# A fused vision network on one core: the other image's sums and norms moved from VectorE and GpSimd to TensorE and ScalarE

## The chip, the cores and the metric

The kernel runs on one core of a Trainium2 chip. The time is that of one execution on the device, in microseconds, taken as a median of several runs. A core has TensorE (matmuls into PSUM), VectorE (DVE in the profile), ScalarE (ACT), GpSimd (POOL) and SyncE (SP, which only issues transfers here); each works through its own queue of instructions in order, and semaphores make them wait for each other.

## The reference

Sixteen images of 48x48 tokens with 96 channels go through two layers, each a state-space block and a feed-forward network with a residual:

```python
# layer 0
x = x + ss2d_0(layernorm(x, 1e-6)) # gate, output product, and a branch: expand, 3x3 depthwise conv, reduce, squeeze-excite
x = x + ffn_0(layernorm(x, 1e-5))
# layer 1
x = x + ss2d_1(layernorm(x, 1e-6)) # layernorm of y over 192 channels, gate, output product
x = x + ffn_1(layernorm(x, 1e-5))

def ss2d(x):
    xc, z = split(x @ in_proj_w.T)                 # 2 x 192 channels
    xc = silu(depthwise3x3(xc) + conv_b)
    xs = [rows(xc), columns(xc), rows(xc)[::-1], columns(xc)[::-1]]    # 4 directions
    dt, B, C = split(x_proj_w @ xs);  delta = softplus(dt_proj_w @ dt + dt_proj_b)
    h[t] = exp(delta[t] * A) * h[t-1] + delta[t] * xs[t] * B[t]        # 16 states per channel
    y[t] = sum over states of h[t] * C[t], + Ds * xs[t]
    y = the four directions added, the column ones turned back
    # layer 1: y = (y - mean) / sqrt(var + 1e-5) * g + b
    return (y * silu(z)) @ out_proj_w.T

def ffn(x):   # operands rounded to 8 bits, sums rounded to fp16
    h = relu(q16(q16(q8(x) @ q8(W1).T) + q8(b1)))
    return q16(q16(q8(h) @ q8(W2).T) + q8(b2))
```

## The kernel before

One image's state is kept in DRAM between its three parts, in one of two sets of buffers. Its scan, `scan` (L461), is the bulk of the work: two pairs of directions, three chunks of 768 tokens, three channel groups j, four row groups i, four state groups g, which is 288 steps in each layer and 9216 in all. A step takes a tile of 128 partitions (32 channels x 4 states) by 768 tokens:

- ScalarE makes `a`, the exp of delta times a rate, in PSUM (L497); `a` has two buffers.
- GpSimd makes `b`, delta u times B (L499), four buffers.
- VectorE scans (L532). In three of four steps the result is written over `a`, and VectorE multiplies it by C to `hc` (L534). In the fourth the result `h` goes to SBUF and GpSimd multiplies.
- ScalarE copies the last column to `carry` for the next chunk (L536).
- TensorE adds the states up: two products per step, issued for two steps together, into `py` (L542), which starts from the skip term (L518) and is copied out every 16 steps (L551).

Beside a scan runs the work of another image, written as Python generators. `together` (L799) takes one scan step and then as much of the other work as keeps it in step: every `yield n` of a generator counts n units, `WORK` has the total of each kind, and the other work is to be spent after 0.94 of the 288 steps. A planner then orders each engine's queue by the program's order as priority and by its own estimate of when operands are ready, so that instructions can be placed ahead of where they stand in the program. The stages are, for images in pairs: the scans of layer 0 beside `final(m-1)` and `first(m+1)`, then beside `middle(m)`; the scans of layer 1 beside `middle(m+1)`, then beside `final(m)` and `first(m+2)`.

- `first` (L769): `before` with layer 0: layernorm (`norm`, L277), transposes (`channels_first`, L298), projections, 3x3 convolutions as nine products with diagonal matrices (`conv`, L329), B and C, delta and delta u.
- `middle` (L772): `merge` (L557), `gate` (L575), `branch` (L599), `add_out` (L654), `feed_forward` (L722) with a norm of its own, and `before` for layer 1.
- `final` (L783): `merge`, `centred` (L686), `gate`, two `add_out`, `feed_forward`.

What the change touches computes as follows before it. `merge` adds the four directions of y, three loaded tiles of [128, 2304] with channels in the partitions, by three additions on GpSimd, two of which read a tile turned (rows and columns of the image swapped, L564 and L566), and one after ScalarE has turned a half tile into `low` (L569, L571). `centred` sums y over channels with matrices of ones (L695), VectorE subtracts the mean from PSUM (L700), ScalarE squares (L701), TensorE sums the squares in columns (L706). In `norm`, VectorE reduces (L281, L289), GpSimd subtracts the mean and multiplies by 1/deviation with broadcast operands (L284, L294). `branch` works in three parts of 128 channels; each part's product is evicted by ScalarE with a bias for part 0 (L632) and added to `t2` by VectorE for parts 1 and 2 (L634). `add_out` adds products out of PSUM to x on VectorE: plainly (L672) or scaled by 1/deviation of each token (L676). In `feed_forward` each sixth of the tokens gets: three products and copies to fp16 by ScalarE (L738), bias and relu by VectorE (L740), a cast to 8 bits by VectorE (L742), nine products (L747), a copy to fp16 by ScalarE (L755), and two additions on GpSimd, of b2 and of the residual (L757, L759).

All evictions of the other work go through `pst` (L272), 2 PSUM buffers:

```python
self.big = pool("big", bufs=5)                                  # tiles of 2304 columns
self.work = pool("work", bufs=2)
self.pq = pool("pq", bufs=2, space=bass.MemoryType.PSUM)        # pst
```

## Time and profile before

| | |
|---|---|
| median of 3 runs | 28,072.75 us (28,056.17 to 28,076.98) |
| the profiled execution's own time | 28,053.55 us |
| its span, first to last instruction | 28,051.8 us |
| first scan, last scan | about 199 us after the start, 178 us before the end |
| mean granted TensorE clock | 0.803 |
| VectorE, GpSimd, TensorE, ScalarE busy | 84%, 83%, 76%, 50% |
| DMA engines busy | 44% on average, 157 GB/s |

A line of the groups reads: line of the code, engine, operation, result and operands with shapes, count, then busy microseconds, mean nanoseconds of one, and the engine's idle time just before these instructions with what ended it. A matmul of fp32 operands has two records. TensorE's busy time includes pipelining and a modelled end, and its clock varies with the stretch: 1.00 in the convolutions, about 0.7 where the scan is alone. A line of the waits reads: who, for whom, microseconds in total, how often, the longest. A line of the windows reads: from and to, length, then each engine's busy time in it with the count of instructions, the granted clock and DMA.

Of the 32 stages, those with `middle` take about 861 us, those with `final` and `first` 867 to 881.

### The profile page before, as it was taken

Reading aid. Unit: us, or ns where it says so; the run is one execution under the profiler, and the core shown is the slowest. Engines: PE = TensorE matmul, PEld = TensorE weight load, DVE = VectorE, ACT = ScalarE, POOL = GpSimd, SP = SyncE. Lnnn points to the kernel's source line nnn. Section 1 sums busy time; section 2 is a strip of 40 time slices with the busy share of each in tenths; the row PEclk is TensorE's granted clock in tenths of the full one; section 3 lists DMA queues with packets and bytes.
Section 4 is the critical chain, followed back from the end, with each engine's and each line's share of the span. In section 5 each row is a group of like instructions: output and inputs, shape, how many; then the busy total and the mean of one; then the engine's idle time right before and its main releaser. Section 6 shows DMA issues by size and latency. Waiting matters only on the chain. (4 is left out here: it accounts for less than half of the span.)

```text
span 28051.8 us, 226543 instructions
## 1 busy us (share of the span) xinstructions
PE 21292.3 (76%) x67072; PEld 7663.6 (27%) x67072; DVE 23442.8 (84%) x18375; ACT 14073.2 (50%) x22285; POOL 23212.7 (83%) x13238
## 2 busy tenths in 40 slices
PE   7777777777778777787777877778777787677876
PEld 2222222222222222232222322223222232222322
DVE  5988888888888888888888888888888888888887
ACT  4455544555445554455444554545545455454553
POOL 5888888887888888888888888888888888888887
PEclk7888878887788777787788877788777887778876
DMA  4444444444444444444444444444444444444443
GB/s 165 151 161 168 152 147 161 167 165 154 149 158 164 163 158 146 156 170 159 162 151 152 165 163 161 150 152 165 160 166 147 150 165 163 163 154 150 162 161 110
DMA packets 1062584, 4406.08 MB, mean 157 GB/s; under 512 B 212064, under 2 KB 212064, under 8 KB 1030368
## 3 DMA queue, kind: packets, MB, share of 16 engines
q1 hardware_dynamic: 869792, 3757.78, 38.2%
q10 hardware_dynamic: 191552, 633.81, 5.7%
q8 instruction: 528, 8.65, 0.1%
q14 instruction: 712, 5.83, 0.1%
HBM read 3499.97 MB, written 891.22 MB: 157 GB/s over the span
## 5 line engine op out<-in xcount | busy, mean ns | idle before, releaser
L499 POOL TENSOR_TENSOR b<-d,bc 128x768 f32<-128x768 f32 x9216 | 16563.8, 1816 | 2899.3 <-DVE a L532 2656.7
L542 PE MATMUL py<-hc,fold_sb 128*32 128x384 f32 x36864 | 11193.0, 620 | 5228.8 <-DVE hc L534 4136.5
L497 ACT ACTIVATE a<-d,l_a 128x768 f32<-128x768 f32 x9216 | 8270.9, 904 | 5410.1 <-DVE h L532 2892.7
L532 DVE TENSOR_TENSOR_SCAN a<-a,carry,b 128x768 f32<-128x768 f32 x4608 | 8257.8, 1814 | 1845.1 <-ACT a L497 966.9
L534 DVE TENSOR_TENSOR hc<-a,bc 128x768 f32<-128x768 f32 x6912 | 6408.5, 945 | 269.1 <-PE py L542 61.4
L542 PEld LDWEIGHTS py<-hc,fold_sb 128*32 128x32 f32 x36864 | 2569.4, 124 | 12738.4 <-DVE hc L534 6589.0
L534 POOL TENSOR_TENSOR hc<-h,bc 128x768 f32<-128x768 f32 x2304 | 4191.1, 1819 | 1239.9 <-DVE h L532 1048.5
L532 DVE TENSOR_TENSOR_SCAN a<-a,b 128x768 f32<-128x768 f32 x2304 | 4003.0, 1753 | 1011.6 <-ACT a L497 516.1
L532 DVE TENSOR_TENSOR_SCAN h<-a,carry,b 128x768 f32<-128x768 f32 x1536 | 2761.6, 1798 | 396.0 <-ACT a L497 355.9
L536 ACT COPY carry<-a 128x1 f32<-128x1 f32 x4608 | 714.7, 156 | 3748.9 <-DVE hc L534 3713.2
L342 PE MATMUL pst<-e,dg 128*128 128x384 f32 x5184 | 1777.2, 490 | 0.0
L532 DVE TENSOR_TENSOR_SCAN h<-a,b 128x768 f32<-128x768 f32 x768 | 1337.3, 1741 | 341.3 <-ACT a L497 156.2
L443 PE MATMUL pst<-dts,wpack_sb 24*128 24x384 f32 x2304 | 1378.5, 726 | 147.9 <-ACT dl L444 146.7
L455 POOL TENSOR_TENSOR du<-dl,u 128x768 f32<-128x768 f32 x576 | 1031.6, 1804 | 328.5 <-ACT dl L448 220.9
L342 PE MATMUL pst<-wxa,dg 128*128 128x384 f32 x3456 | 1218.5, 497 | 27.3 <-DMA dg<-taps_l0a 23.1
L342 PEld LDWEIGHTS pst<-e,dg 128*128 128x128 f32 x5184 | 959.0, 189 | 788.3 <-issue 153.7
L444 ACT ACTIVATE dl<-pst,wpack_sb 128x384 f32<-128x384 f32 x1152 | 654.1, 577 | 858.9 <-PE pst L443 685.4
L425 PE MATMUL pst<-u,wpack_sb 128*24 128x384 f32 (+1 forms) x2304 | 890.5, 513 | 37.9 <-ACT row L429 19.3
L342 PE MATMUL pst<-wxb,dg 128*128 128x384 f32 (+1 forms) x2304 | 879.9, 509 | 3.6 <-ACT wxb L374 3.6
L551 ACT COPY yt<-py 128x768 f32<-128x768 f32 x576 | 459.5, 798 | 726.1 <-PE py L542 724.7
L443 PEld LDWEIGHTS pst<-dts,wpack_sb 24*128 24x128 f32 x2304 | 526.4, 260 | 1073.9 <-ACT dl L444 516.0
L342 PEld LDWEIGHTS pst<-wxa,dg 128*128 128x128 f32 x3456 | 623.9, 189 | 622.8 <-issue 226.1
(147 smaller groups left out, 15581.5 us busy)
## 6 DMA issues: line engine op xcount, KB each, us to landing
d<-dd SPq DMA_DIRECT2D x2304, 768.0 KB, 4.6
bc<-bc SPq DMA_DIRECT2D x1536, 768.0 KB, 5.0
dd<-dl ACTq DMA_DIRECT2D x192, 1152.0 KB, 4.7
dd<-du SPq DMA_DIRECT2D x576, 384.0 KB, 2.7
y<-yt ACTq DMA_DIRECT2D x576, 384.0 KB, 2.3
u<-u ACTq DMA_DIRECT2D x96, 1152.0 KB, 4.9
first<-u SPq DMA_DIRECT2D x288, 384.0 KB, 3.1
first<-y SPq DMA_DIRECT2D x288, 384.0 KB, 3.2
```

The lines of the kernel that those rows point to most:

```text
L342: nc.tensor.matmul(img(o[:, :SUB]), lhsT=dg[:n, k, :], rhs=img(p[:n], PW)[:, PQ * q + i : PQ * q + i + PQ, j : j + HW], start=(k == 0), st ...
L425: nc.tensor.matmul(o[:m, :SUB], lhsT=w[:, j, :], rhs=u[j][:, cs], start=(j == 0), stop=(j == 2))
L443: nc.tensor.matmul(o[:, :SUB], lhsT=dtw[:, col, :], rhs=dts[:, cs], start=True, stop=True)
L444: nc.scalar.activation(dl[:, cs], o[:, :SUB], AF.Identity, bias=self.get(t + "dtb")[:, col : col + 1])
L455: nc.gpsimd.tensor_tensor(du, dl[:, cs], u[j][:, cs], ALU.mult)
L497: nc.scalar.activation(a, d[:, 0, :], AF.Exp, scale=rates[:, pair, j, i, g : g + 1])
L499: nc.gpsimd.tensor_tensor(b, d[:, 1, :], bc[:, 0, :], ALU.mult)
L532: nc.vector.tensor_tensor_scan(way(h), way(a), way(b), start, ALU.mult, ALU.add)
L534: (nc.vector if here else nc.gpsimd).tensor_tensor(hc, h, cc, ALU.mult)
L536: nc.scalar.copy(carry[:, at : at + 1], h[:, last : last + 1])
L542: nc.tensor.matmul(py[at : at + 32, q, :SUB], lhsT=self.fold, rhs=hcs[k][:, q * SUB : (q + 1) * SUB], start=False, stop=(g == GROUPS - 1),)
L551: nc.scalar.copy(sub(yt), py[:, :, :SUB])
```

## The change

No part of the scan is changed. Of the other image's work:

- `merge` becomes sums on TensorE, in pieces of 384 tokens: identity times the first tile, plus halves of the identity times turned slices of the others, evicted by ScalarE.
- `centred` no longer calls `merge`: it has a constant `centre` of four 128x192 blocks, identity less 1/192, which merge and centre in one group of four products; ScalarE squares out of PSUM and copies.
- `norm` subtracts and scales by ScalarE, one activation of 96 columns for each of the 18 token groups, with the mean as bias and then 1/deviation as scale.
- `channels_first` casts to 8 bits on ScalarE.
- `branch` adds `t2` by a product with the identity; ScalarE evicts.
- `add_out` adds x by a product with the identity; the scaled products are first scaled by ScalarE into `y2` and added the same way; `final` calls it once instead of twice.
- `feed_forward`: bias and relu on ScalarE; b2 and the residual each by a pair of products and an eviction by ScalarE.
- The units and `WORK` follow: 192, 461, 152 for 201, 464, 151.

```diff
     def norm(self, x, eps):
-        nc.vector.tensor_scalar_mul(m, m, 1.0 / DM)
+        nc.vector.tensor_scalar_mul(m, m, -1.0 / DM)
+        yield 2
         xm = self.bigt([128, NT, DM], "xm")
-        nc.gpsimd.tensor_tensor(xm, x, m.unsqueeze(2).broadcast_to([128, NT, DM]), ALU.subtract)
-        yield 6
+        for i in range(NT):
+            nc.scalar.activation(xm[:, i, :], x[:, i, :], AF.Identity, bias=m[:, i : i + 1])
+            if i % 3 == 2:
+                yield 0.8
...
-        nc.gpsimd.tensor_tensor(xm, xm, r.unsqueeze(2).broadcast_to([128, NT, DM]), ALU.mult)
-        yield 4
+        yield 1
+        for i in range(NT):
+            nc.scalar.activation(xm[:, i, :], xm[:, i, :], AF.Identity, scale=r[:, i : i + 1])
+            if i % 3 == 2:
+                yield 0.8
...
-                nc.vector.tensor_copy(out, p[:DM, :SUB], saturate=False)
+                nc.scalar.activation(out, p[:DM, :SUB], AF.Identity, saturate=False)
...
     def merge(self, s):
-        nc.gpsimd.tensor_tensor(img(y[0][:64]), img(y[0][:64]), swapped(y[2][:64]), ALU.add)
-        yield 5.5
-        nc.gpsimd.tensor_tensor(img(y[0][64:]), img(y[0][64:]), swapped(y[1][64:]), ALU.add)
-        yield 5.5
-        low = self.bigt([64, L], "low")
-        nc.scalar.copy(img(low), swapped(y[2][64:]))
-        yield 1
-        nc.gpsimd.tensor_tensor(y[1][:64], y[1][:64], low, ALU.add)
-        yield 5.5
+        for q in range(NQ):
+            cs, rows = slice(q * SUB, (q + 1) * SUB), slice(q * PQ, (q + 1) * PQ)
+            o = self.pst()
+            nc.tensor.matmul(o[:, :SUB], lhsT=self.ident, rhs=y[0][:, cs], start=True, stop=False)
+            nc.tensor.matmul(img(o[:64, :SUB]), lhsT=low, rhs=turned[2][:, rows], start=False, stop=True)
+            nc.tensor.matmul(img(o[64:, :SUB]), lhsT=high, rhs=turned[1][:, rows], start=False, stop=True)
+            nc.scalar.copy(y[0][:, cs], o[:, :SUB])
+            yield 2
+        for q in range(NQ):
...
+            nc.tensor.matmul(o[:64, :SUB], lhsT=low, rhs=y[1][:, cs], start=True, stop=False)
+            nc.tensor.matmul(img(o[:64, :SUB]), lhsT=high, rhs=turned[2][:, rows], start=False, stop=True)
+            nc.scalar.copy(y[1][:64, cs], o[:64, :SUB])
+            yield 1.4
...
     def branch(self, ya, yb):
+                if m > 0:
+                    nc.tensor.matmul(
+                        o[:DM, :SUB], lhsT=self.ident[:DM, :DM], rhs=t2[:, cs], start=True, stop=False
+                    )
...
-                    nc.vector.tensor_tensor(t2[:, cs], o[:DM, :SUB], t2[:, cs], ALU.add)
+                    nc.scalar.copy(t2[:, cs], o[:DM, :SUB])
...
     def add_out(self, x, terms, scaled=(), scale=None):
+            if scaled:
+                o = self.pst()
+                self.products(o, q, scaled, True)
+                y = self.work.tile([128, TQ * DM], F32, name="y2", tag="w1")
                 for i in range(TQ):
                     at = TQ * q + i
-                    nc.vector.scalar_tensor_tensor(
-                        xq[:, i, :],
+                    nc.scalar.activation(
+                        y[:, i * DM : (i + 1) * DM],
                         o[:, i * DM : (i + 1) * DM],
...
+            o = self.pst()
+            for k, y in enumerate(added):
+                nc.tensor.matmul(o[:, : TQ * DM], lhsT=self.ident, rhs=y, start=k == 0, stop=False)
+            self.products(o, q, terms, False)
+            nc.scalar.copy(xq, o[:, : TQ * DM])
             yield TQ * len(terms) / 2
...
     def centred(self, s):
+            for n, into, sq, at in ((128, y[0], sqa, 0), (64, y[1], sqb, 128)):
+                o = self.pst()
+                for k, rhs in enumerate((img(y[0][:, cs]), img(y[1][:, cs]), turned[1][:, rows], turned[2][:, rows])):
+                    nc.tensor.matmul(
+                        img(o[:n, :SUB]),
+                        lhsT=self.centre[:, k, at : at + n],
+                        rhs=rhs,
+                        start=(k == 0),
+                        stop=(k == 3),
+                    )
+                outs.append((o, n, into, sq))
+            for o, n, into, sq in outs:
+                nc.scalar.activation(sq[:, cs], o[:n, :SUB], AF.Square)
+                nc.scalar.copy(into[:n, cs], o[:n, :SUB])
+            yield 5
...
     def feed_forward(self, t, x):
-                nc.vector.tensor_scalar(h1[:, m, :], h1[:, m, :], b1[:, m : m + 1], 0.0, ALU.add, ALU.max)
+                nc.scalar.activation(h1[:, m, :], h1[:, m, :], AF.Relu, bias=b1[:, m : m + 1])
...
-            nc.gpsimd.tensor_tensor(y1, y1, b2.unsqueeze(1).broadcast_to([128, TQ, DM]), ALU.add)
-            xs = x[:, TQ * q : TQ * (q + 1), :]
-            nc.gpsimd.tensor_tensor(xs, xs, y1, ALU.add)
-            yield 1.5
+            o = self.pst()
+            nc.tensor.matmul(o[:, : TQ * DM], lhsT=self.ident16, rhs=y1, start=True, stop=False)
+            nc.tensor.matmul(o[:, : TQ * DM], lhsT=self.ones16, rhs=b2, start=False, stop=True)
+            y1 = self.work.tile([128, TQ * DM], F16, name="y1")
+            nc.scalar.copy(y1, o[:, : TQ * DM])
+            yield 0.5
+            o = self.pst()
+            xs = x[:, TQ * q : TQ * (q + 1), :].rearrange("p s c -> p (s c)")
+            nc.tensor.matmul(o[:, : TQ * DM], lhsT=self.ident, rhs=xs, start=True, stop=False)
+            nc.tensor.matmul(o[:, : TQ * DM], lhsT=self.ident16, rhs=y1, start=False, stop=True)
+            nc.scalar.copy(xs, o[:, : TQ * DM])
+            yield 1
...
-WORK = {"first": 201, "middle": 464, "final": 151}
+WORK = {"first": 192, "middle": 461, "final": 152}
```

## The prediction

> **What bounds the kernel now.** I read the table of engines first, then the costliest groups, then who waits for whom on VectorE, and last the busy times stage by stage, since the average over the span hides which engine is full where.
>
> ```profile
> PE 21292.3 (76%) x67072; PEld 7663.6 (27%) x67072; DVE 23442.8 (84%) x18375; ACT 14073.2 (50%) x22285; POOL 23212.7 (83%) x13238
> ...
> L499 POOL TENSOR_TENSOR b<-d,bc 128x768 f32<-128x768 f32 x9216 | 16563.8, 1816 | 2899.3 <-DVE a L532 2656.7
> L532 DVE TENSOR_TENSOR_SCAN a<-a,carry,b 128x768 f32<-128x768 f32 x4608 | 8257.8, 1814 | 1845.1 <-ACT a L497 966.9
> L534 DVE TENSOR_TENSOR hc<-a,bc 128x768 f32<-128x768 f32 x6912 | 6408.5, 945 | 269.1 <-PE py L542 61.4
> L534 POOL TENSOR_TENSOR hc<-h,bc 128x768 f32<-128x768 f32 x2304 | 4191.1, 1819 | 1239.9 <-DVE h L532 1048.5
> ```
>
> The kernel is 9216 scan steps. Four steps give VectorE four scans (about 1.78 us) and three products (0.945), 10.0 us, so 2.5 us a step; they give GpSimd five products of 1.82, 2.3 us a step. With nothing else to do a step takes 2.5 us, and VectorE is the bound with GpSimd close behind. 9216 x 2.5 is 23,040 us; the ends without a scan take some 200 us before the first and 178 after the last. The other 4,600 us of the span are what the work of the other image adds, about 145 us in each of the 32 stages.
>
> ```profile
> DVE a L532 <- ACT a L497: 1483.0, 1336, 10.6
> DVE a L532 <- ACT carry L536: 1157.8, 1062, 9.0
> DVE h L532 <- ACT a L497: 512.1, 183, 11.8
> ...
> DVE xs L672 <- PE pst L662: 149.8, 38, 8.3
> DVE y L700 <- PE pst L695: 142.6, 21, 23.6
> ```
>
> VectorE's idle time ends mostly on ScalarE (3.2 ms), seldom on GpSimd. ScalarE is half idle, but its queue is in order: an eviction that waits for TensorE holds back the exp behind it. That is the danger of a change that adds evictions. The stages say where it matters. First a stage with `middle` (columns: TensorE, its weight loads, VectorE, ScalarE, GpSimd busy, then clock and DMA): merge, branch part 0, branch parts 1 and 2, output sum, norm with transposes, feed-forward.
>
> ```profile
> 11462.90:11499.00 36.10, 16.64 (x45) 4.11 (x44) 29.66 (x23) 15.88 (x23) 36.10 (x17) 0.69 0.56 186
> ...
> 11547.40:11608.30 60.90, 57.64 (x196) 23.05 (x196) 56.96 (x43) 30.11 (x58) 53.97 (x34) 1.00 0.40 144
> 11608.30:11753.00 144.70, 142.14 (x511) 64.26 (x512) 137.92 (x108) 73.78 (x134) 124.81 (x73) 1.00 0.45 156
> 11778.40:11820.60 42.20, 38.40 (x161) 22.75 (x160) 31.13 (x30) 14.46 (x17) 26.89 (x16) 0.74 0.37 131
> 11820.60:11853.80 33.20, 21.87 (x71) 7.40 (x72) 32.55 (x30) 15.05 (x17) 30.86 (x17) 0.71 0.34 119
> 11853.80:11921.00 67.20, 42.78 (x156) 11.06 (x155) 63.90 (x59) 29.69 (x56) 55.03 (x37) 0.75 0.30 106
> ```
>
> Then one with `final` and `first`: merge, centring, output sums, norm with transposes, feed-forward.
>
> ```profile
> 13184.00:13210.20 26.20, 12.53 (x39) 3.28 (x36) 23.37 (x18) 14.82 (x21) 26.20 (x14) 0.76 0.62 223
> 13210.20:13263.60 53.40, 45.34 (x152) 21.59 (x152) 40.76 (x39) 20.57 (x41) 43.39 (x23) 0.79 0.43 149
> ...
> 13295.20:13401.30 106.10, 83.02 (x314) 37.53 (x314) 97.54 (x93) 46.20 (x84) 90.73 (x52) 0.84 0.36 126
> 13401.30:13450.90 49.60, 25.96 (x92) 8.12 (x89) 46.81 (x39) 22.65 (x40) 44.51 (x24) 0.69 0.36 135
> 13450.90:13563.10 112.20, 66.12 (x232) 17.73 (x232) 109.91 (x93) 46.15 (x73) 94.27 (x60) 0.71 0.40 135
> ```
>
> Merge is full on GpSimd (36.1 of 36.1), feed-forward and norm on VectorE (63.9 of 67.2, 109.9 of 112.2), the branch on TensorE (142 of 145, at clock 1.00). Dividing each window's scan time by 1.77 gives its steps; its length less 2.5 us a step is what its other work costs. Middle: merge 7, output sum 12, norm and transposes 6, feed-forward 20. Final: merge and centring 19, output sums 10, norm 8, feed-forward 17. These 99 us in a pair of stages are what the change can win at most, about 1.6 ms of the span. The second norm (4 to 5 in each), gate, convolutions, projections and delta products make up the rest.
>
> [...] The relu (L740) shows it here: 283 ns at least, 765 median, 1975 at most. So removing it frees its mean of 805 ns, not 283, and I go by 805. [...] The turned copy (L569) took 4143 ns where an activation of as many elements in line (L590) took 2124. No row here shows a turned operand on TensorE: that price is open from none to double.
>
> **The change part by part.** Per stage, in us, plus is a gain.
>
> *Merge, middle.* GpSimd loses 6.2 + 6.2 + 5.0, ScalarE a copy of 4.1; the first add runs ahead in the tail of the stage before, so some 11 lie in the window. TensorE gets 30 sums of 384 columns at about 0.64 (two records of about 320 ns at full clock: the convolution's 5184 records, 1777 us), 19 us, and ScalarE 12 evictions of 0.48. In 12 steps TensorE's own fold takes about 12 us, in all 31 of the present 36. So 5 are won if turned columns run at full rate; 18 of the 30 sums are turned, and doubled they cost 11.5. I take the middle, 6: gain 0, ends -7 and +6.
>
> *Branch.* VectorE loses 12 adds of 543 ns (6.5), TensorE gets 12 x 0.64 = 8. Parts 1 and 2 go at 144.7 us for 55.7 steps, 2.60 a step; part 0, whose eviction is ScalarE's already, at 2.60 too. TensorE is the bound, so VectorE's adds were hidden and the sums are not: -5, ends -8 and 0.
>
> *Output sum, middle.* Six sums of 288 columns, 0.5 each, where TensorE is full (38 of 42), against six adds of 451 ns: -1, ends -3 and +3.
>
> *Norms, two in every stage.* GpSimd loses 2 x 3.08; ScalarE gets 36 activations of 96 columns. Near rows are 274 ns (128x96, L174) and 310 (with a bias operand, L291), so 10 to 11 us on a queue that has 15 of 33 busy. The two reductions of 1.94 stay on VectorE. ScalarE just fits while it also makes the exps, but in bursts: 0, ends -4 and +4 each. The transposes' six casts of 540 ns leave a VectorE that is full: +3.
>
> *Feed-forward.* VectorE loses 18 x 0.805 = 14.5, GpSimd 6 x 1.48 = 8.9. The cast of 1.0 stays. ScalarE gets 18 relus at about 0.58 (L444) and 12 evictions at 0.40: 15. TensorE gets some 5. In the middle stage ScalarE would have 45 us in a window of 53, 85% with three round trips to TensorE in each sixth: I take 9 of 14.5. In the final stage it has 61 of 98: 11. Ends 0 and 14.5.
>
> *Merge and centring, final.* GpSimd loses 17.4, VectorE 12 x 0.53 = 6.4, TensorE's two kinds of row sums go (12 x 0.64) and 48 come, net 36 x 0.64 = 23. With the column sums (about 18) and the fold TensorE has some 75 to 80 us in today's 79.6; the excess of 19 shrinks to some 5 if turned operands are free, and 24 of them doubled add 15. Gain 10, ends -3 and +16.
>
> *Output sums, final.* VectorE loses 18 x 0.302 + 6 x 0.451 = 8.1 where it has 97.5 of 106; ScalarE gets as much and has half its time free, TensorE 12 x 0.5. Gain 6, ends 0 and 8.
>
> *At nothing:* the constants (a few VectorE instructions before the first image), and the new totals, which spread 344 units instead of 352 and leave `middle` at 461 for 464; the loads on SP's queue are the same three and stand at the same place, so no queue is passed. The cover of nothing else changes.
>
> The sum: middle 0 - 5 - 1 + 3 + 9 = 6; final 10 + 6 + 3 + 11 = 30. 16 x 6 + 15 x 30 = 546 us. At the ends nothing hides the new work: the first norm about +6, the last image's centring on TensorE (31 us for about 22) and two more round trips in each sixth of its feed-forward, some 25 together. Net 515 of the profiled execution's 28,053.6, which is 19 under the median of the runs: 27,540 to 27,560, I say 27,550, 1.9% faster. What is late next in merge and branch is TensorE, in feed-forward ScalarE.
>
> **Rivals.**
> *ScalarE's queue takes the gain back (slower).* New tiles that ScalarE must wait for: 12 + 12 + 6 + 6 + 12 = 48 in a middle stage, 12 + 12 + 6 + 12 = 42 in a final one, some 1,440. Today VectorE's 3.2 ms of idle behind ScalarE, over some 5,300 evictions (the counts of its groups that read PSUM, without the scan's), is 0.6 us each. At that price the change pays 870 us more and ends near 28,420. It decides from 0.36 us each on. For it: two PSUM buffers only, and the chain of three evictions in the feed-forward. Against it: part 0 of the branch is made of just such evictions (L626, L632) and goes at 2.60 a step.
>
> *Turned sums at half speed (still faster).* All at double: 6 and 8 worse, 16 x 14 = 224 us back: about 27,770.
>
> *The stages keep their pace.* The planner orders the queues by its own estimates; if VectorE's new gaps are filled by waits for ScalarE at just the old rate, nothing moves: 28,050.
>
> **How the numbers follow.** The forecast 0.47, its own range 27,250 to 27,700; more than it, down to 27,000, 0.08; turned sums slow 0.12; no change 0.07; slower 0.26. Change of 0.2% is about what a measurement of this kernel can tell. Faster 0.67, same 0.07, slower 0.26. Leaving out 0.07 below and 0.13 above, the range is 27,080 to 28,430.
>
> **What would show it.** Right: GpSimd's busy falls by about 1.2 ms, VectorE's by about 0.9, ScalarE's rises by 1.4 to 1.6; the feed-forward windows shrink to about 58 and 101 us; the granted clock rises in the merge. Wrong: feed-forward steps stay at 3.5 with VectorE idle behind L497; merge's turned matmuls well over 0.64; waits of ScalarE for TensorE grow by a millisecond and VectorE's idle with them; the branch longer by over 8.

## The result and the profile after

The changed kernel takes 28,179.6 us (median of 5 runs, 28,168.2 to 28,206.3) where the kernel before, beside it, takes 28,056.2: a ratio of 1.0045, 95% interval 1.0031 to 1.0060. It is slower by 0.45%. The forecast was 27,550, faster by 1.9%; the time lies inside the range (27,080 to 28,430), on the side that had 0.26. The profiled execution took 28,188.6 us, its span is 28,186.8.

The page of the kernel after, the engines' busy times and four of the costliest groups (the same rows as those of before; the lines of the file have moved: L499 is L527, L532 is L560, L534 is L562, L497 is L525, L536 is L564):

```profile
PE 22314.0 (79%) x71104; PEld 8071.8 (29%) x71104; DVE 22762.0 (81%) x16758; ACT 15421.2 (55%) x26764; POOL 22014.6 (78%) x12630
...
L527 POOL TENSOR_TENSOR b<-d,bc 128x768 f32<-128x768 f32 x9216 | 16561.0, 1816 | 3706.7 <-DVE a L560 3594.9
...
L560 DVE TENSOR_TENSOR_SCAN a<-a,carry,b 128x768 f32<-128x768 f32 x4608 | 8264.5, 1814 | 2302.4 <-ACT a L525 1434.1
...
L562 DVE TENSOR_TENSOR hc<-a,bc 128x768 f32<-128x768 f32 x6912 | 6442.2, 948 | 551.4 <-PE py L570 257.7
...
L562 POOL TENSOR_TENSOR hc<-h,bc 128x768 f32<-128x768 f32 x2304 | 4191.3, 1819 | 1730.9 <-DVE h L560 1372.4
```

The work went where the change put it: GpSimd lost 1,198 us of busy time, VectorE 681, ScalarE gained 1,348 and TensorE 1,022. The scan's own instructions cost what they did (1,814, 948 and 1,816 ns). What grew is the last field: the large group of scans waits 2,302 us where it waited 1,845, and the exp of ScalarE (L525) is what ends most of that.

So I keep one account in the rest of this text. The span is the time that VectorE, the bound, is busy plus the time that it idles (span less busy):

| | VectorE busy | VectorE idle | span |
|---|---|---|---|
| before | 23,442.8 | 4,609.0 | 28,051.8 |
| after | 22,762.0 | 5,424.8 | 28,186.8 |
| difference | -680.8 | +815.8 | +135.0 |

The 681 us that were taken from VectorE came back as idle time, and 135 more. Who waits for whom on VectorE says on whom (waiter, releaser, then us in total, how often, the longest):

```profile
DVE a L560 <- ACT a L525: 2265.4, 1709, 22.8
DVE a L560 <- ACT carry L564: 1264.0, 1063, 8.6
DVE h L560 <- ACT a L525: 266.0, 244, 11.8
...
DVE hq L803 <- ACT h L801: 139.7, 54, 11.8
DVE m L303 <- ACT xs L735: 114.2, 17, 79.0
```

The first row was 1,483 us, 1,336 times. All waits of VectorE for ScalarE sum to 4,586 us (before 3,470), those for TensorE and GpSimd to 485 (before 861). And ScalarE's own waits for TensorE went from 3,877 to 5,563 us. The rows suggest a chain: the exp of the next step stands in ScalarE's queue behind an eviction, and the eviction waits for a sum of TensorE. One such case stands in the output sums shown below: ScalarE begins to scale a sum (L723) at 13,388.3 us, after 6.32 us of waiting for TensorE (L703), its next exp begins 0.5 us later, and the scan that needs it ends an idle time of VectorE of 5.86 us. How much of the new idle time that chain makes is what the experiments had to show.

The stretches of two stages, cut at the same instructions as those shown of before. First a middle stage: merge, feed-forward, and the norm behind it; then a final one: merge with centring, output sums, feed-forward (columns: TensorE, its weight loads, VectorE, ScalarE, GpSimd busy, then clock and DMA):

```profile
11505.30:11551.00 45.70, 40.09 (x116) 10.12 (x114) 37.45 (x29) 21.75 (x43) 35.79 (x20) 0.92 0.51 182
11910.40:11982.10 71.70, 48.18 (x191) 15.11 (x191) 59.00 (x44) 44.37 (x93) 49.76 (x28) 0.82 0.32 114
11982.10:12002.20 20.10, 10.60 (x31) 2.33 (x29) 16.72 (x15) 17.61 (x44) 11.39 (x7) 0.75 0.61 210
13239.10:13334.40 95.30, 89.22 (x279) 37.61 (x277) 65.63 (x50) 41.60 (x83) 62.46 (x35) 0.88 0.43 145
13363.00:13435.20 72.20, 65.87 (x249) 34.61 (x250) 48.45 (x37) 31.26 (x68) 51.14 (x30) 0.83 0.35 120
13483.40:13595.40 112.00, 72.81 (x274) 21.57 (x271) 102.79 (x80) 64.22 (x122) 94.55 (x53) 0.83 0.39 133
```

In merge with centring TensorE has 89 of 95 us, in the output sums 66 of 72, and VectorE only 66 and 48. In the small norm window ScalarE has 17.6 of 20.1. Three stretches have a new bound. Stretches hold different numbers of scan steps in the two kernels, so what follows compares their excess: the length less 2.5 us for each step that ran in it, mean over the 16 middle stages and over 14 final ones. How a step is counted that a window cuts moves a row by up to 1.7 us, so rows that differ by less than 2 us say nothing.

| excess in us | before | after |
|---|---|---|
| middle: merge | 7.7 | 7.5 |
| middle: branch | 19.4 | 23.2 |
| middle: output sum | 9.4 | 9.5 |
| middle: norm and transposes | 5.6 | 5.5 |
| middle: feed-forward | 19.7 | 16.4 |
| middle: the norm behind it | 4.5 | 7.6 |
| middle: delta products | 36.3 | 45.7 |
| final: merge and centring | 18.4 | 28.0 |
| final: gate | 12.7 | 4.5 |
| final: output sums | 11.6 | 21.2 |
| final: norm and transposes | 6.8 | 3.9 |
| final: feed-forward | 18.9 | 11.9 |
| stage in all, middle and final | 860.9, 876.2 | 869.4, 871.5 |

The delta products are the same instructions in both kernels and cost 9.4 us more in each middle stage, which is 150 us in 16 stages and more than the whole difference of the two kernels. That row asked for experiments of its own. The end after the last scan grew from 178 to 227 us.

### The profile page after: what moved, and what is told of

It is laid out like the page before. It is cut to its first block, busy times and chain, and to the rows that moved or that the text cites. A ratio compares the mean times of both kernels' runs of the same rounds, so it can differ in the third digit from the quotient of the medians.

```text
span 28186.8 us, 237117 instructions
## 1 busy us (share of the span) xinstructions
PE 22314.0 (79%) x71104; PEld 8071.8 (29%) x71104; DVE 22762.0 (81%) x16758; ACT 15421.2 (55%) x26764; POOL 22014.6 (78%) x12630
## 3 DMA queue, kind: packets, MB, share of 16 engines
q1 hardware_dynamic: 869792, 3757.78, 38.2%
## 5 line engine op out<-in xcount | busy, mean ns | idle before, releaser
L527 POOL TENSOR_TENSOR b<-d,bc 128x768 f32<-128x768 f32 x9216 | 16561.0, 1816 | 3706.7 <-DVE a L560 3594.9
L570 PE MATMUL py<-hc,fold_sb 128*32 128x384 f32 x36864 | 10751.0, 599 | 4477.3 <-DVE hc L562 3579.1
L525 ACT ACTIVATE a<-d,l_a 128x768 f32<-128x768 f32 x9216 | 8267.4, 904 | 3739.7 <-DVE h L560 1878.4
L560 DVE TENSOR_TENSOR_SCAN a<-a,carry,b 128x768 f32<-128x768 f32 x4608 | 8264.5, 1814 | 2302.4 <-ACT a L525 1434.1
L562 DVE TENSOR_TENSOR hc<-a,bc 128x768 f32<-128x768 f32 x6912 | 6442.2, 948 | 551.4 <-PE py L570 257.7
L570 PEld LDWEIGHTS py<-hc,fold_sb 128*32 128x32 f32 x36864 | 2466.1, 122 | 11655.9 <-DVE hc L562 5732.7
L562 POOL TENSOR_TENSOR hc<-h,bc 128x768 f32<-128x768 f32 x2304 | 4191.3, 1819 | 1730.9 <-DVE h L560 1372.4
L560 DVE TENSOR_TENSOR_SCAN a<-a,b 128x768 f32<-128x768 f32 x2304 | 4011.6, 1755 | 1339.3 <-ACT a L525 831.3
L560 DVE TENSOR_TENSOR_SCAN h<-a,carry,b 128x768 f32<-128x768 f32 x1536 | 2767.0, 1801 | 347.7 <-ACT a L525 229.5
L564 ACT COPY carry<-a 128x1 f32<-128x1 f32 x4608 | 717.7, 157 | 2804.9 <-DVE hc L562 2792.7
L560 DVE TENSOR_TENSOR_SCAN h<-a,b 128x768 f32<-128x768 f32 x768 | 1337.5, 1741 | 307.3 <-POOL b L527 142.0
L751 PE MATMUL pst<-y,centre 128*64 128x384 f32 (+1 forms) x1536 | 813.9, 674 | 16.5 <-DMA y<-y 16.3
```

The source lines that it names most:

```text
L525: nc.scalar.activation(a, d[:, 0, :], AF.Exp, scale=rates[:, pair, j, i, g : g + 1])
L527: nc.gpsimd.tensor_tensor(b, d[:, 1, :], bc[:, 0, :], ALU.mult)
L560: nc.vector.tensor_tensor_scan(way(h), way(a), way(b), start, ALU.mult, ALU.add)
L562: (nc.vector if here else nc.gpsimd).tensor_tensor(hc, h, cc, ALU.mult)
L564: nc.scalar.copy(carry[:, at : at + 1], h[:, last : last + 1])
L570: nc.tensor.matmul(py[at : at + 32, q, :SUB], lhsT=self.fold, rhs=hcs[k][:, q * SUB : (q + 1) * SUB], start=False, stop=(g == GROUPS - 1),)
```

## The experiments

After the result I held this theory: a part of the forecast's gains is there, and ScalarE's new evictions take more than that back (Q, the rival of the prediction). Against it stood that the price lies in TensorE's turned reads, in the norm's bursts on ScalarE, or in no part of the change at all but in where its totals put the other work.

Parts of the change were undone one at a time in the changed kernel, later put alone into the kernel before. A time is to be read against 28,180 in the first group and against the kernel before beside it (28,027 to 28,064) elsewhere; ratios are always to the kernel before. The last three of the first group ran beside a kernel before of 28,027.3 us, 29 less than beside the changed kernel; where it matters, the difference by the ratios is given too. Excesses of further kernels are counted like those of the table or by the share of each step that lies in the window; the two differ by less than 2 us.

### Which part costs, which pays

**The output sums of before, in the changed kernel.**

```diff
-            for k, y in enumerate(added):
-                nc.tensor.matmul(o[:, : TQ * DM], lhsT=self.ident, rhs=y, start=k == 0, stop=False)
-            self.products(o, q, terms, False)
-            nc.scalar.copy(xq, o[:, : TQ * DM])
+                nc.vector.tensor_tensor(xq, o[:, : TQ * DM], xq, ALU.add)
...
+                    nc.vector.scalar_tensor_tensor(xq[:, i, :], o[...], scale[:, at : at + 1], xq[:, i, :], ALU.mult, ALU.add)
```

> The changed kernel (28,180 us) with the output sums of before: VectorE adds and scales out of PSUM again, in two passes in final. Theory Q (an eviction that waits for TensorE stands in ScalarE's queue ahead of the exp, so VectorE's scan is late): 27,950 to 28,050, as the output sums cost 9.6 us more in each final stage than before and TensorE's waits for them (L735 615 us, L723 306 us on ScalarE) go. Theory T (TensorE has too much to do): the same or a little less, since only 18 sums of 288 columns go: 28,050 to 28,120. Theory P (ScalarE is simply busier, the waits do not matter): 28,180 to 28,300, because VectorE gets some 170 us of work back.

28,247.3 us, ratio 1.0074 (1.0059 to 1.0089): 67 us slower than the changed kernel. Theory Q fell here; the time lies in theory P's range. In its surroundings the changed form of the output sums pays, if little: a final stage is 2.9 us shorter without it, a middle one 6.0 longer. It isn't where the time went.

**The sums stay on TensorE, VectorE evicts them.**

```diff
-                    nc.scalar.activation(y[...], o[...], AF.Identity, scale=scale[:, at : at + 1])
+                    nc.vector.tensor_scalar_mul(y[...], o[...], scale[:, at : at + 1])
...
-            nc.scalar.copy(xq, o[:, : TQ * DM])
+            nc.vector.tensor_copy(xq, o[:, : TQ * DM])
```

> The changed kernel with one thing altered: the output sums stay on TensorE with the identity, in one pass, but their evictions (scaling into y2, copy to x) are made by VectorE, not ScalarE. Theory Q: most of what undoing the part brings, 27,970 to 28,090, since the waits for TensorE leave ScalarE's queue. Theory T: no change, 28,150 to 28,250, since TensorE's sums are all there and VectorE gets 170 us more. Theory P: 28,120 to 28,180.

28,192.4, ratio 1.0052 (1.0037 to 1.0067), within 13 us of the changed kernel. VectorE is busy 121 us longer and idles 127 less (5,297.5). Theory Q, which wanted 27,970 to 28,090 us, fell again; the time lies in theory T's range. For these sums it makes no difference which of the two engines evicts.

**Merge and centring of before, in the changed kernel.**

```diff
-            nc.tensor.matmul(o[:, :SUB], lhsT=self.ident, rhs=y[0][:, cs], start=True, stop=False)
-            nc.tensor.matmul(img(o[:64, :SUB]), lhsT=low, rhs=turned[2][:, rows], start=False, stop=True)
...
+        nc.gpsimd.tensor_tensor(img(y[0][:64]), img(y[0][:64]), swapped(y[2][:64]), ALU.add)
...
-                    nc.tensor.matmul(img(o[:n, :SUB]), lhsT=self.centre[:, k, at : at + n], rhs=rhs, ...)
...
+                nc.vector.scalar_tensor_tensor(y[:, cs], o[:n, :SUB], -1.0 / DI, y[:, cs], ALU.mult, ALU.add)
...
-WORK = {"first": 192, "middle": 461, "final": 152}
+WORK = {"first": 192, "middle": 458, "final": 154}
```

> The changed kernel with merge and centring of before (GpSimd's three additions, VectorE's subtraction of the mean). Theory T with slow turned operands: 27,950 to 28,050, for the merge with centring has 28 us of excess in a final stage against 18 before, and TensorE is full there (89 of 95 us). Theory Q: 28,080 to 28,180, the evictions there wait only 282 us in all. If GpSimd's additions are dearer than they looked: 28,200 to 28,350.

28,029.8, ratio 0.9993 (0.9984 to 1.0002): 150 us faster. The final stage's excess in this part goes from 28.0 back to 20.4. But a final stage as a whole is only 2.9 us shorter, since its gate and its output sums get longer, and some 98 of the 150 us come from the middle stages (869.4 to 863.3), where the merge's excess hardly changes and that of the branch, in which nothing was edited, falls by 8.6. The totals had to follow here too. So this run doesn't give the price of the part; the run with operands in line, below, is the better evidence.

**The feed-forward of before, in the changed kernel.**

```diff
-                nc.scalar.activation(h1[:, m, :], h1[:, m, :], AF.Relu, bias=b1[:, m : m + 1])
+                nc.vector.tensor_scalar(h1[:, m, :], h1[:, m, :], b1[:, m : m + 1], 0.0, ALU.add, ALU.max)
...
-            (b2 and the residual as two pairs of products, each evicted by ScalarE)
+            nc.gpsimd.tensor_tensor(y1, y1, b2..., ALU.add)
+            nc.gpsimd.tensor_tensor(xs, xs, y1, ALU.add)
```

> The changed kernel with the feed-forward of before (relu on VectorE, b2 and residual on GpSimd; norm and transposes stay changed). The windows say that this part gained 3 us in a middle stage and 7 in a final one: 28,300 to 28,400 if that gain is its own. Theory Q says that its three evictions in a row cost elsewhere (the planner puts them among the exps): then 28,100 to 28,200.

28,365.1, ratio 1.0114 (1.0099 to 1.0129): 185 us slower, as expected if its gain is its own, and against theory Q. This part pays.

**The norm of before, in the changed kernel.**

```diff
-        for i in range(NT):
-            nc.scalar.activation(xm[:, i, :], x[:, i, :], AF.Identity, bias=m[:, i : i + 1])
+        nc.gpsimd.tensor_tensor(xm, x, m.unsqueeze(2).broadcast_to([128, NT, DM]), ALU.subtract)
...
-WORK = {"first": 192, "middle": 461, "final": 152}
+WORK = {"first": 189, "middle": 455, "final": 149}
```

> The changed kernel with the norm of before: GpSimd subtracts and scales with broadcast operands, two instructions of 3.08 us instead of 36 activations of 0.36. (The units' totals follow: 189, 455, 149.) Theory P (bursts of ScalarE's own work hold the exps back, no wait for TensorE needed): 27,950 to 28,080. If the norm is a fair exchange: 28,150 to 28,210. If GpSimd's broadcasts are dearer: 28,250 or more.

27,985.1, ratio 0.9984 (0.9978 to 0.9991): 195 us faster (166 by the ratios), all of it in the middle stages (869.4 to 856.5). The totals had to follow the norm's units, so a part of it may be theirs. Nearest to direct evidence is the norm behind the feed-forward. Its window with the norm of before:

```profile
11884.40:11905.10 20.70, 11.26 (x30) 2.45 (x28) 20.24 (x17) 11.39 (x17) 18.58 (x10) 0.75 0.74 231
```

VectorE has 20.2 of 20.7 us where it had 16.7 of 20.1, and ScalarE 11.4 where it had 17.6: the excess there falls from 7.6 to 3.8. In this window of the changed kernel 18 activations of 361 ns follow each other for 4.9 us without an exp of the scan among them; in the norm ahead of the feed-forward exps stand between runs of 3 to 9. But these 4 us are a third of what a middle stage gains. Of the rest, 7.7 lie in the branch, which has no edit, as in the run with merge and centring of before; and in the final stages the windows of both norms are 3 to 4 us longer with the norm of before. So how much of the 195 is the norm's own isn't shown.

**Turned operands read in line.** The sums, evictions and units stay; only the addresses of the turned operands become those of the untouched image. The image isn't turned back, so this kernel leaves out that part of the computation. VectorE, ScalarE and GpSimd have the same instructions in the same order in both traces, and TensorE too, but for 24 of 71,104 records that changed places with a neighbour. So it is the reads that differ.

```diff
-        turned = [swapped(yj) for yj in y]
+        turned = [img(yj) for yj in y]
```

> The changed kernel with every turned operand of merge and centring read in line instead (the image is not turned back, so y is not the reference's; counts, shapes and waits stay). Theory T (the turned reads fill TensorE): most of what undoing merge and centring brought (150 us), so 28,030 to 28,090. If the sums cost by their number and their place, whatever the read: 28,150 to 28,190. The turned records (829 ns mean against 566 in line) should fall to about 560.

27,915.1, ratio 0.9961 (0.9947 to 0.9975): 265 us faster (236 by the ratios), close to 1% of the kernel for a way of reading, more than expected, and enough by itself to decide between slower and faster than before. The excess of merge falls from 7.5 to 1.6 in the middle stages, that of merge with centring from 28.0 to 18.1 in the final ones; the end after the last scan is 14 us shorter. Over all stages that comes to some 260 us. First the groups of the changed kernel, shapes apart, then the same of this one (busy us, mean ns of one record; a product has two records):

```profile
L751 PE MATMUL pst<-y,centre 128*128 128x384 f32 x768 | 423.3, 688 | 16.5 <-DMA y<-y 16.3
L751 PE MATMUL pst<-y,centre 128*64 128x384 f32 x768 | 398.6, 659 | 0.0
...
L602 PE MATMUL pst<-y,ident 128*64 128x384 f32 x192 | 139.4, 829 | 0.0
```

```profile
L751 PE MATMUL pst<-y,centre 128*128 128x384 f32 x768 | 300.8, 524 | 13.3 <-DMA y<-y 13.3
L751 PE MATMUL pst<-y,centre 128*64 128x384 f32 x768 | 276.7, 496 | 0.0
...
L602 PE MATMUL pst<-y,ident 128*64 128x384 f32 x192 | 79.1, 507 | 0.0
```

L602 is 96 products: 1.45 us each turned, 0.82 in line. In L751 half of the 768 products are turned, and the 244 us between the two kernels are 0.64 for each of these 384. A turned product costs 0.63 to 0.64 us more, some 424 us of TensorE's time for all 672 of them, of which 265 show in the kernel's.

**The branch's additions back on VectorE.**

```diff
-                    nc.scalar.copy(t2[:, cs], o[:DM, :SUB])
+                    nc.vector.tensor_tensor(t2[:, cs], o[:DM, :SUB], t2[:, cs], ALU.add)
```

> The changed kernel with the branch's sum t2 of before: VectorE adds out of PSUM, no product with the identity. The prediction's step (TensorE is full in the branch, so the sums cost 5 us a middle stage and VectorE's adds were hidden): 28,080 to 28,130. If the exchange is even: 28,160 to 28,200. If VectorE's adds are not hidden: 28,250.

28,185.9, ratio 1.0058 (1.0043 to 1.0073): 6 us from the changed kernel, 35 by the ratios, whose intervals overlap. No difference between the sum on TensorE and the addition on VectorE is shown.

### The totals

**The kernel before with other totals.** Not one instruction of the computation differs; `together` spreads the other work a little differently over the scan steps; a larger total draws it earlier. The new totals here are the sums of the kernel's own `yield`s. So the kernel before had a margin of 12 units over its sums in `first` and in `middle`, and the change, whose totals are the sums of its own, dropped that margin.

```diff
-WORK = {"first": 201, "middle": 464, "final": 151}
+WORK = {"first": 189, "middle": 452, "final": 151}
```

> The kernel before with only the units' totals changed to the true sums of its own yields (189, 452, 151 for 201, 464, 151), so that the other work ends at 0.94 of the steps as it does in the changed kernel. Theory W (the totals, which I had put at nothing, move the delta products to a worse place: dt windows of 36 us excess became 46): 28,130 to 28,230. If the totals are indifferent: 28,020 to 28,080.

28,299.8, ratio 1.0099 (1.0084 to 1.0115): 1% slower. VectorE's busy time stays (23,467), its idle time grows by 208 us. The middle stages take 883.0 instead of 860.9 (the final ones 867.5 instead of 876.2), and 14 of these 22 us lie in the output sum: an excess of 23.4 instead of 9.4. Ten us at a time, this is the kernel before at the end of its branch and in its output sum (the column before the last two is TensorE's granted clock):

```profile
11760.00:11770.00 10.00, 8.34 (x33) 3.65 (x32) 9.80 (x9) 4.11 (x5) 8.78 (x6) 1.00 0.19 68
11770.00:11780.00 10.00, 6.31 (x20) 2.71 (x22) 8.81 (x9) 4.09 (x6) 7.22 (x5) 0.58 0.40 150
11780.00:11790.00 10.00, 10.00 (x32) 6.56 (x29) 1.92 (x2) 3.31 (x4) 1.46 (x1) 0.50 0.10 39
11790.00:11800.00 10.00, 10.00 (x40) 5.67 (x39) 8.20 (x8) 2.26 (x3) 5.73 (x4) 0.73 0.32 114
11800.00:11810.00 10.00, 10.00 (x59) 6.42 (x58) 10.00 (x10) 3.36 (x5) 8.76 (x6) 1.00 0.67 245
```

and this the same stretch with the smaller totals:

```profile
11870.00:11880.00 10.00, 7.10 (x24) 1.95 (x22) 9.71 (x8) 4.87 (x6) 8.55 (x5) 1.00 0.52 202
11880.00:11890.00 10.00, 8.45 (x27) 4.85 (x27) 6.66 (x7) 5.71 (x7) 5.47 (x4) 0.54 0.31 114
11890.00:11900.00 10.00, 10.00 (x28) 5.99 (x28) 4.45 (x5) 0.90 (x1) 1.80 (x1) 0.50 0.15 61
...
11910.00:11920.00 10.00, 10.00 (x28) 5.31 (x28) 6.40 (x6) 1.90 (x3) 7.14 (x4) 0.50 0.24 79
11920.00:11930.00 10.00, 10.00 (x33) 6.70 (x34) 5.40 (x6) 2.57 (x3) 1.81 (x1) 0.50 0.03 7
```

When the branch ends, the clock falls to half in both: in the first during 5.0 us without a matmul, in the second in two rows of which TensorE had nothing to do for 4.45 us. In the first kernel it is back at 1.00 after 24 us, in the second it stays at 0.50 for 51 us, until the output sum is over; TensorE does 28 to 33 matmuls in 10 us where the first does 40 and 59 as its clock rises, and VectorE, which adds these sums to x, works 4.5 to 6.7 of 10 us in these rows. Over the 16 middle stages the clock in the output sum is 0.81 on average in the first and 0.57 in the second. In the two runs of the sweep below with 6 units less and 6 more it is 0.68, and the excess 22.5 and 23.5.

**The changed kernel with its totals raised by 12.**

```diff
-WORK = {"first": 192, "middle": 461, "final": 152}
+WORK = {"first": 204, "middle": 473, "final": 152}
```

> The changed kernel with its units' totals raised to 204, 473 and 152, the same distance over the true sums as the kernel before had (201, 464, 151 for 189, 452, 151), so that the other work runs ahead by as much. Theory W (the 272 us that true totals cost the kernel before are part of what the change cost too): 27,880 to 28,050. If the totals only hurt the old mix of work: 28,150 to 28,210.

28,443.4, ratio 1.0137 (1.0122 to 1.0153): 264 us slower than the changed kernel, although the margin of 12 units is back; theory W's 27,880 to 28,050 fell. Neither "more units are better" nor "fewer" holds; it is a matter of where things fall.

**Norm, merge and centring of before in the changed kernel, at two totals.** The edits of the two experiments above together, and the first or the second of these lines:

```diff
+WORK = {"first": 201, "middle": 464, "final": 151}
...
+WORK = {"first": 189, "middle": 452, "final": 151}
```

> The changed kernel with norm, merge and centring of before and the totals of before (201, 464, 151; the true sums are those of before): what is left of the change is feed-forward, transposes, output sums and the branch's sum. If the three costs add up (150 for merge and centring, 195 for the norm, up to 270 for the totals): 27,560 to 27,700. If they are one cost seen three times: 27,900 to 28,000.

27,975.5, ratio 0.9971 (0.9960 to 0.9981): the three costs don't add up.

> The same parts as in the run before this one, with the true totals 189, 452, 151. If norm and merge add up (150 and 195): 27,830 to 27,880; the totals are the rest. If they overlap: 27,950 to 28,000.

28,187.4, ratio 1.0047 (1.0032 to 1.0062), outside both expectations. Both kernels have the norm, merge and centring of before, and 12 units decide between faster and slower than before.

The delta products sort the kernels of this text. Their excess in a middle stage is 36.6 to 37.2 us in the five that have the totals 201 and 464 over the sums 189 and 452 (the kernel before, the first of these two, and the three under "Parts alone" below), and 42 to 53 in all fifteen others, whatever their edits. It goes with the totals and not with a part of the change.

**A sweep of both kernels** (the totals of `first` and `middle` in units from each kernel's own; `final` stays):

> The kernel before with its totals for the first and middle stages at 195 and 458 (it has 201 and 464; at 189 and 452 it took 28,300). Theory W (the totals place the rest of the work, each kernel scatters by half a per cent and more over them): anything from 27,900 to 28,300, not on a line between the two known points. Theory V (more units is simply later work, a smooth slope): 28,150 to 28,200, halfway.

> The kernel before with totals 207 and 470. Theory W: 27,900 to 28,350. Theory V: the slope of the two known points goes on, 27,930, or has its floor at 28,050.

> The changed kernel with totals 198 and 467 (it has 192 and 461; at 204 and 473 it took 28,443). Theory W: 28,000 to 28,450, with at least one point of the changed kernel at or below 28,100. Theory V: halfway, 28,310, and the changed kernel above the kernel before at each point.

> The changed kernel with totals 210 and 479. Theory W: 28,000 to 28,500. Theory V: the slope goes on, 28,570 or more.

```diff
-WORK = {"first": 201, "middle": 464, "final": 151}
+WORK = {"first": 195, "middle": 458, "final": 151}
...
+WORK = {"first": 207, "middle": 470, "final": 151}
...
-WORK = {"first": 192, "middle": 461, "final": 152}
+WORK = {"first": 198, "middle": 467, "final": 152}
...
+WORK = {"first": 210, "middle": 479, "final": 152}
```

| totals | time | VectorE busy | VectorE idle |
|---|---|---|---|
| before, less 12 | 28,299.8 | 23,467 | 4,817 |
| before, less 6 | 28,426.6 | 23,392 | 5,053 |
| before, its own | 28,054 | 23,443 | 4,609 |
| before, plus 6 | 28,402.1 | 23,517 | 4,881 |
| after, its own | 28,179.6 | 22,762 | 5,425 |
| after, plus 6 | 28,406.7 | 22,751 | 5,654 |
| after, plus 12 | 28,443.4 | 22,740 | 5,702 |
| after, plus 18 | 28,545.6 | 22,764 | 5,780 |

Theory V, a smooth slope, fell with the first row between two known points. Theory W was right that the times scatter and overlap, and too mild: 28,426.6, 28,402.1 and 28,545.6 lie outside its limits, and it wanted a point of the changed kernel at 28,100 or below, which there isn't. The changed kernel's four points do rise all the way, as theory V had it, though not evenly. The kernel before stands on a low point with 250 to 370 us more on either side.

The rows pair by their margin over the sums of the `yield`s, 0, 6, 12 and 18 in each half of the table. At equal margins the changed kernel is 120 us faster, 20 faster, 389 slower and 144 slower. The measured +0.45% compares margin 12 with margin 0.

Over four totals each, the means of the times are 28,296 and 28,394: 98 us apart, less than either kernel's own scatter. What doesn't scatter so far is the account: VectorE's busy time is 701 us less in the mean of the changed kernels, and its idle time 800 more, the smallest idle of the changed kernels (5,425) above the largest of the others (5,053). So the trade, some 700 us for some 800, is the change's own at these totals; whether the net is a gain or a loss depends on the totals.

### Parts alone in the kernel before

**The changed feed-forward alone, at the totals of before.**

```diff
-                nc.vector.tensor_scalar(h1[:, m, :], h1[:, m, :], b1[:, m : m + 1], 0.0, ALU.add, ALU.max)
+                nc.scalar.activation(h1[:, m, :], h1[:, m, :], AF.Relu, bias=b1[:, m : m + 1])
...
-            nc.gpsimd.tensor_tensor(y1, y1, b2.unsqueeze(1).broadcast_to([128, TQ, DM]), ALU.add)
-            nc.gpsimd.tensor_tensor(xs, xs, y1, ALU.add)
+            (the two pairs of products and evictions of the change)
```

> The kernel before, totals untouched, with the feed-forward of the change alone (relu on ScalarE, b2 and residual as sums on TensorE). If its gain of 185 us in the changed kernel is its own: 27,820 to 27,900. If it needs the other parts, or the planner spoils it: 28,000 to 28,100.

27,795.2, ratio 0.9903 (0.9889 to 0.9918): 269 us faster than the kernel before. The gain is its own.

**Only the relu on ScalarE.** One line; bias b2 and residual stay on GpSimd.

```diff
-                nc.vector.tensor_scalar(h1[:, m, :], h1[:, m, :], b1[:, m : m + 1], 0.0, ALU.add, ALU.max)
+                nc.scalar.activation(h1[:, m, :], h1[:, m, :], AF.Relu, bias=b1[:, m : m + 1])
```

> The kernel before with the relu of the feed-forward on ScalarE alone; bias and residual stay on GpSimd. The changed feed-forward as a whole took 27,795 against 28,054. Theory S (the gain is GpSimd's freed time, 800 additions that no longer delay the scan's products): the relu alone changes nothing, 28,000 to 28,100. Theory R (the gain is VectorE's freed time[...]): 27,900 to 27,950. Theory W (placement): any value by half a per cent, slower included.

27,681.0, ratio 0.9863 (0.9847 to 0.9879): 376 us faster than before, 499 faster than the changed kernel, and faster than all else that ran. Theory R was right in kind, and its gain of 100 to 150 us too small by more than half: the trace of before has 576 relus of 0.805 us in the mean, 455.8 us of VectorE's time. The relu of before, then of this kernel (minimum, median, maximum in ns):

```profile
L740 DVE TENSOR_SCALAR h<-h,l_b x576: 283/765/1975, 1444.5 to 28041.7; 128x384 f16<-128x384 f16 x192
```

```profile
L740 ACT ACTIVATE h<-h,l_b x576: 598/616/651, 1441.4 to 27676.8; 128x384 f16<-128x384 f16 x192
```

and the page and the two feed-forward windows of this kernel:

```profile
PE 21014.5 (76%) x67072; PEld 7602.8 (27%) x67072; DVE 23075.5 (83%) x17799; ACT 14336.3 (52%) x22861; POOL 23248.0 (84%) x13238
```

```profile
11707.70:11769.80 62.10, 39.62 (x156) 10.98 (x155) 52.18 (x41) 37.65 (x74) 55.44 (x37) 0.79 0.33 115
13293.00:13387.60 94.60, 55.87 (x217) 15.68 (x216) 89.74 (x68) 51.67 (x88) 86.76 (x55) 0.77 0.50 167
```

VectorE's busy time fell by 367 us and its idle time by nothing (4,609.0 to 4,611.6): the span fell by 365. The excess of the feed-forward goes from 19.7 to 12.9 and from 18.9 to 9.3; in the middle stages every other row of the table above stays within 0.4 us. This is what all of the change was to do, and the relu alone does it; it reads and writes SBUF, and ScalarE has no wait just before it in the trace, while the copies ahead of it (L738) wait 95.4 us for TensorE. That busy time and span agree to 2 us is in part luck, though. A middle stage is 7.3 us shorter, almost all of it in the feed-forward; a final stage is 17.5 shorter, about half of it in the feed-forward and the rest in windows without an edit (delta products, output sums, the second norm). And the relu was tried at one setting of the totals only.

**Feed-forward and output sums together, at the totals of before.**

```diff
-        yield from self.add_out(x, [(ya, self.ow1["g", "a"]), (yb, self.ow1["g", "b"])], r)
-        yield from self.add_out(x, [(za, self.ow1["b", "a"]), (zb, self.ow1["b", "b"])])
+        yield from self.add_out(x, [(za, ...), (zb, ...)], [(ya, ...), (yb, ...)], r)
```

> The kernel before with the changed feed-forward and the changed output sums; merge, centring, norms, branch and casts as before. Theory A (the parts' gains add): the output sums were worth 67 us in the changed kernel, so 27,700 to 27,750. Theory W (the totals place the rest): the sums make the units of the final stage last differently, 27,650 to 28,100, with no relation to 67.

27,986.4, ratio 0.9974 (0.9963 to 0.9984): 191 us slower than with the feed-forward alone. Gains don't add (theory A fell): the same output sums that were worth 67 us in the changed kernel cost 191 here. The windows of a final and a middle stage's output sum, and who waits for whom in the first:

```profile
13261.40:13321.80 60.40, 56.99 (x241) 30.78 (x241) 38.63 (x30) 27.29 (x61) 42.09 (x25) 0.94 0.29 105
11740.10:11778.30 38.20, 38.20 (x167) 22.47 (x167) 25.28 (x20) 12.70 (x19) 23.36 (x14) 0.84 0.42 145
```

```profile
ACT xs L697 <- PE pst L665: 17.7, 6, 4.5
POOL b L505 <- DVE a L538: 12.5, 6, 4.5
ACT y L685 <- PE pst L665: 11.7, 6, 2.4
DVE a L538 <- ACT a L503: 9.6, 3, 5.6
DVE a L538 <- ACT carry L542: 8.4, 3, 5.0
```

TensorE is full (57.0 of 60.4, 38.2 of 38.2), ScalarE waits 29 of 60 us for these sums, and VectorE idles 18 for the exp and the carry, which stand in ScalarE's queue. Not all of the 191 is that: the norm that follows in the middle stages, the same instructions in both kernels, has an excess of 11.5 instead of 5.6, which is some 94 us in 16 stages and comes from where it now falls.

The way from before to after, in the order in which these kernels contain each other:

| step | span | VectorE busy | VectorE idle |
|---|---|---|---|
| relu to ScalarE | -365 | -367 | +3 |
| b2 and residual as sums | +109 | -6 | +115 |
| output sums | +196 | -97 | +293 |
| merge, centring, norms, branch, casts, totals | +194 | -211 | +405 |

## Why the prediction was wrong

*The sum.* A middle stage was to get 6 us shorter and is 8.5 longer (860.9 to 869.4); a final one was to get 30 shorter and is 4.7 shorter (876.2 to 871.5); the ends were to cost 25 and cost 49. What was to leave VectorE and GpSimd left them. Three steps failed: the floor under merge and centring, the waits that were kept out of the sum, and the totals.

*Merge and centring, final: forecast +10 a stage, measured about -10.* The forecast said that TensorE would have 75 to 80 us in a window of 79.6, and then that the excess would shrink to 5. The two don't go together: the window holds 24.5 steps, 61 us, and a TensorE of 75 to 80 leaves an excess of 14 to 19. In line TensorE has 78 us and the excess is 18.1, just that; with turned operands it has 89 and the excess is 28.0. A window that is handed to another engine has that engine's time as its floor.

*The waits.* The forecast counted what leaves VectorE and GpSimd as gain where they were full, with discounts, and priced the new waits only in a rival. Measured, the busy time fell by 681 us and the new idle time was 816. The rival of ScalarE's queue had put 870 on it, at 0.6 us for each of 1,440 new tiles to wait for; it belonged in the forecast's own sum. That 870 is close to 816 is in part luck, for its one price is no law: put into the kernel before one after the other, the 384 evictions of the feed-forward's sums cost 0.3 us of idle each, the 288 of the output sums 1.0 (with the norm that they displaced), the 576 relus nothing. In the changed kernel undoing the output sums gains nothing, and neither does evicting them with VectorE. And some 30% of the new idle comes from how long TensorE reads turned operands (the run in line idles 248 us less).

*Turned operands.* They cost 0.63 to 0.64 us more each, against the 0.64 at which the forecast priced a product: the double end of its range. By the groups that is 15 us in a final stage and 11 in a middle one, as the forecast had written down for that end; the excess shows 9.9 and 5.9 of it. The forecast had only a turned copy of ScalarE to go by and left open whether TensorE pays for such an operand; the row of L602 (829 ns a record, 507 in line) shows that it does. The rival of turned sums put 224 us on the way from its middle to double; the whole way from in line to double is 424 us by the same figures, and 265 were measured, since not all of TensorE's time is on the path.

*Merge, middle: 0, measured 0.2.* Right as far as the count of steps tells, with the turned reads in it (5.9 of the excess).

*Feed-forward: 9 and 11 a stage, some 310 us in all.* Right in kind and too much: 269 alone in the kernel before, 185 in the changed one, where the windows' excess falls by 3.3 and 7.0. Its parts were weighed wrongly: the relu alone gives 376, and with the sums, taken to be free on a half idle ScalarE, 114 of that is gone. That a relu taken away frees its mean of 805 ns was the forecast's estimate from the row of L740, and too much, as VectorE's busy time fell by 367, 0.64 each.

*Norms: 0, ends -4 and +4 for each of two.* The activations take 361 ns, not 274 to 310:

```profile
L321 ACT ACTIVATE xm<-xm,r 128x96 f32<-128x96 f32 x1152 | 328.5, 361 | 2.0 <-DVE r L318 1.8
L308 ACT ACTIVATE xm<-xs,m 128x96 f32<-128x96 f32 x1152 | 328.1, 361 | 18.0 <-DVE m L304 14.6 <-POOL du L483 3.1 <-issue 0.3
```

Of the two rows behind the 274 and 310, one has no bias operand (L174) and the other only 18 columns (L291), so neither had the norms' form. The run with the norms of before is 166 to 195 us faster, but how much of that is the norms' isn't shown.

*Output sums: +6 and -1, 74 us.* 67 by the first experiment, -191 by the last. The worth of this part depends on what stands around it, so that 67 lies near 74 is luck.

*The transposes' casts: +3.* No run undoes them alone.

*Branch: -5.* Undoing its sum gains nothing that could be shown, within the ends. The branch's excess is 3.8 longer after all, and stays so with VectorE adding (23.0): it isn't the sum on TensorE.

*The totals: at nothing.* The forecast saw the totals fall by 9 and 3 units, and not that a margin of 12 over the sums of the `yield`s went with them. Twelve units are some 250 to 270 us in either kernel, half of the forecast's whole gain. The delta products, whose excess grew by 9.4 us in each middle stage of the changed kernel with no edit in them, grow by 11.4 in the kernel before when only its totals are changed. That alone is more than what the middle stages lost.

*The ends: +25, measured +49.* Twice as much, all of it after the last scan. (546 less 25 is 521, not 515; the 6 us decide nothing.)

*What would show it.* GpSimd's 1.2 ms came out as said. VectorE's 0.9 was 0.68. The feed-forward windows did not come to 58 and 101 us (71.7 and 112.0). ScalarE's waits for TensorE grew by 1.7 ms and VectorE's idle time with them, which had been named as a sign of being wrong, as had turned products well over 0.64.

What stays open: how far the +0.45% is the change's and how far it is its totals'. The trade of busy for idle time is the change's own; the balance of the two is smaller than what the totals move. The costs of the parts neither add up nor stay the same from one kernel to the other, so the 630 us between forecast and result can't be shared out among the three steps. Nor was it separated why the totals move the excess of the delta products. For the output sum of the kernel before, its length goes with TensorE's clock (38.2 us at 0.94 and 42.2 at 0.74 with its own totals, 46.0 at 0.67 and 51.2 at 0.53 with the smaller ones); why the clock stays down is open.

## What to carry to other kernels

Write a change to a kernel with one full engine as two sums, what leaves that engine and what idle it gets from the queue that feeds it, and forecast their difference; here one line that moved to the feeding engine without a round trip to a third one gave about its busy time (1.4%, at one setting of the totals), while sums that make the feeding engine wait for a matmul gave less than nothing in the kernel before (114 and 191 us lost). Give every window the new engine's own time as its floor before taking a gain from it. And where other work is spread over a pipeline by hand-set totals, shift them in the old kernel first, and compare the two kernels at the same margin: if a shift moves the time by as much as the change is to bring, one setting of each says little.

## What the runs showed of the hardware

- TensorE's granted clock stayed at half in a stretch that the profile shows as fully busy. With the smaller totals it was 0.50 for 51 us with TensorE busy 10.0 of 10 in most of it and VectorE waiting for it; with the totals of before it fell during 5.0 us without a matmul and was back at 1.00 after 24 us. The stretch at 0.50 holds small products of 96 columns with a weight load each, and what kept the clock down there was not separated by any run.
- A moving operand that is read with rows and columns exchanged took 1.45 us busy in a product of 384 columns, against 0.82 for the same product read in line (L602): 0.63 us more.
- A relu of 128x384 took 283 to 1,975 ns on VectorE and 598 to 651 on ScalarE. Of the 576 on VectorE, the 49 in whose time GpSimd had no instruction took 304 to 321 ns; the other 527 had a median of 782. The slower engine by the minimum was the better place.
